# A cross-attention kernel whose statements are all put into another order

## The chip, the cores and the metric

The kernel runs on one NeuronCore of a Trainium2 chip. The metric is device time in microseconds of one launch that does the whole computation; the kernel before takes 1358.28 us (median of 3 runs, 1357.85 to 1358.52). The core's engines run at the same time, each its own instructions in order: TensorE (PE, with weight loads PEld), VectorE (DVE), ScalarE (ACT), GpSimd (POOL), and SyncE (SP), which only issues transfers here. They wait for one another through semaphores.

## What is computed

Cross-attention of 64 batches, in float32. x holds 256 rows of 512 for each batch, the context c 256 rows of 384.

```python
Q = layer_norm(x @ W_text + b_text, g1, beta1)        # 256 x 512
V = c @ W_audio + b_audio                             # 256 x 512
K = layer_norm(V, g2, beta2)
alpha = softmax(Q @ K.T / sqrt(512))                  # 256 x 256
H = (alpha @ V) @ W_out + b_out
out = layer_norm(H + x, g_out, beta_out)
```

The kernel folds W_audio @ W_out into one matrix (`wao`), so that the output is alpha @ c @ wao plus a bias row.

## The kernel before, in words

Batches are worked on one behind the other in a pipeline. A first part written out by hand takes batches up to 5 into the pipeline, then 58 steady rounds run (`for b in range(3, B - 3)`, line 1825), then an end written out by hand empties it. In round b five batches are in work: `q2` and `k2` project batch b+2; `at` is the attention of batch b up to the softmax; `last` (b-1) takes alpha @ c; `old` (b-2) multiplies with `wao` and adds x (`y` is its product); `settled` (b-3) does the last layer norm.

Nearly every matrix product is computed with fewer block products than the plain way, from sums and differences of blocks. The query projection is a `Fork` of 7 block products (`one` to `seven`, line 733); the key projection and the output product are `Thirds` of 15 products of 171 columns (`one` to `five`, line 557), whose blocks M, L, T, U, N lie in three PSUM banks, and between whose groups VectorE or ScalarE moves partial sums (`copy_n1`, `start_t`, `copy_t`, `start_l0`, `start_l1`, `take_m`, `start_u`). The scores are 7 parts (`score_part`, line 884), the context 7 parts and 2 plain products (`z_part`, line 1000, `context_two`, line 1062). The operands' sums are made mostly by GpSimd (`query_step`, `key_step`, `c_step`, `e_step`, `cs[..].add`, `x_new.add`, `z_step`).

The names that the prediction's steps touch:

- `at.add_p7(0)` and `(1)` (line 541): VectorE adds the kept seventh score part to scores in PSUM. `score_part(5)` waits for the first of them.
- `settled.shift(t)` (line 1261) and `settled.settle(t)` (line 1270): VectorE's two passes of the last layer norm over a row tile of 512; both read two tensors in SBUF: the row and a vector.
- `turn_c`, `turn_x`, `turn_e`, `k.turn`, `q.turn` (lines 76 and 520): VectorE turns 32x32 squares; the transfer that loaded them has put the squares in place.
- `y.one` needs all `z_step`s that make its operands; `y.three` needs `y.start_t`, and that `y.copy_n1` on ScalarE; `y.five` needs `y.take_m`.
- `store_e`, `fetch_e`: alpha goes to DRAM and comes back as squares (`ed`, `eq`); the same for keys (`kd`, `kq`) and queries (`qd`, `qq`).

The order is the order of the statements: the compiler's own scheduling is switched off (`tc.manual_schedule()`), every engine runs its instructions as the program issues them, and the first thing that waits holds up what stands behind it on its engine. All transfers in the rounds are issued on SP's queue, also in order. So a statement's place sets both where it stands on its own engine and what it stands behind.

Of the kernel before, what the change touches and what calls it, by code (L numbers as in the profile page):

```python
# [15 lines left out]
P = 128  # L16
# [6 lines left out]
def kernel(  # L23
# [1288 lines left out]

    keep_busy(6)
    c_turn = RowTurn(c_0, AC, 'cT')
    c_turn.tile(0)
    c_turn.tile(1)
    k[0] = Projection('k', 0, c_turn.T, wa_sb, ba_sb, AC, ST, bank[0:2])
    k[0].multiply(0, [0])
    k[0].multiply(1, [0])
    war = []  # L1320
    pool, tag = (once, 'e')
    war.append(pool.tile([P, HC, P], F32, tag=tag, name=f'war_{0}'))
    arrange(war[0], wa_sb[:, 0, :], HC, nc.gpsimd.tensor_copy)
    mean_wa = means(wa_sb, AC, 'mwa')
    k[0].multiply(0, [1])
    k[0].multiply(0, [2])
    k[0].multiply(1, [1])
    x_turn = RowTurn(x_0, DC, 'xT')
    x_turn.tile(0)
    k[0].multiply(1, [2])  # L1330
    pool, tag = (work, 'eT')
    war.append(pool.tile([P, HC, P], F32, tag=tag, name=f'war_{1}'))
    arrange(war[1], wa_sb[:, 1, :], HC, nc.gpsimd.tensor_copy)
    x_turn.tile(1)
    mean_wt = means(wt_sb, DC, 'mwt')
    pool, tag = (work, 'eT')
    war.append(pool.tile([P, HC, P], F32, tag=tag, name=f'war_{2}'))
    arrange(war[2], wa_sb[:, 2, :], HC, nc.gpsimd.tensor_copy)
    centre(wa_sb, mean_wa, AC)
    wa_t = const.tile([P, 11, WP], F32, tag='wa_thirds', name='wa_thirds')  # L1340
    third_weights(wa_sb, wa_t, [0])
    turn_weights(0, 1)
    k[0].evict(0)
    k[0].evict(1)
    q[0] = Projection('q', 0, x_turn.T, wt_sb, bt_sb, DC, LT, bank[2:4])
    q[0].multiply(0, [0])
    q[0].multiply(0, [1])
    cT[1] = turn_c(1)
    turn_weights(1, 1)
    bt_row = bt_sb.rearrange('p (o h) -> p o h', o=1)  # L1350
    mean_bt = means(bt_row, 1, 'mbt')
    q[0].multiply(1, [0])
    q[0].multiply(1, [1])
    k[0].scales()
    k[0].normalise([0])
    q[0].multiply(0, [2])
    q[0].multiply(0, [3])
    q[0].multiply(1, [2])
    q[0].multiply(1, [3])
    k[0].normalise([1])  # L1360
    k[0].store()
    turn_weights(2, 1)
    centre(wt_sb, mean_wt, DC)
    wt_blocks = weight_sums(wt_sb, DC // 2, 'wtsum')
    turn_weights(3, 1)
    centre(bt_row, mean_bt, 1)
    k[1] = Projection('k', 1, cT.pop(1), wa_sb, ba_sb, AC, ST, bank[4:6])
    k[1].multiply(0, [0])
    q[0].evict(0)
    q[0].evict(1)  # L1370
    k[1].multiply(0, [1])
    q[0].scales()
    xT[1] = turn_x(1)
    k[1].multiply(0, [2])
    k[1].multiply(1, [0])
    ba_row = ba_sb.rearrange('p (o h) -> p o h', o=1)
    mean_ba = means(ba_row, 1, 'mba')
    load_c(2)
    k[1].multiply(1, [1])
    fold_multiply(1, 0, 1)  # L1380
    fold_multiply(0, 0, 1)
    q[0].normalise([0])
    q[0].normalise([1])
    q[0].store()
    k[1].multiply(1, [2])
    bt_step = const.tile([P, H2], F32, tag='bt_step', name='bt_step')
    nc.vector.tensor_tensor(bt_step, bt_sb[:, :H2], bt_sb[:, H2:], ALU.subtract)
    g1_sb, be1_sb, g2_sb, be2_sb, bac_sb = take_columns()
    fold_multiply(1, 1, 2)
    fold_multiply(1, 2, 3)  # L1390
    load_x(2)
    centre(ba_row, mean_ba, 1)
    xs_1 = SumX(xT.pop(1), nc.vector)
    xs_1.add(1)
    fold_multiply(1, 3, 4)
    k[1].evict(0)
    Fork.seed()
    xs_1.add(1)
    k[1].evict(1)
    part = bias_parts()  # L1400
    xs[1] = xs_1
    q[1] = Fork(1, xs.pop(1).of, wt_blocks)
    q[1].one()
    q[1].seven()
    xs_1.add(1)
    k[1].square()
    wa_blocks = third_weights(wa_sb, wa_t, [3])
    q[1].after_one()
    fold_multiply(0, 1, 2)
    q[1].six()  # L1410
    ba_delta = third_bias(ba_sb, 'ba_delta')
    bias_rest(part, 1, 2)
    nc.vector.tensor_scalar(g2_sb, g2_sb, scale, None, ALU.mult)
    k[1].scales()
    k[1].normalise([0])
    cT[2] = turn_c(2)
    cs[2] = Sides(cT.pop(2), 'csum')
    cs[2].add(1)
    k[0].fetch()
    xs_1.add(1)  # L1420
    q[0].fetch()
    q[1].after_seven()
    q[1].start_q3()
    folds.append(p_at.tile([P, H], F32, tag='at', name='ps_fold'))
    fold_multiply(2, 0, 1)
    cs[2].add(1)
    cs[2].add(1)
    fold_multiply(0, 2, 3)
    cs[2].add(1)
    cs[2].add(1)  # L1430
    q[1].step_r()
    q[1].five()
    k[1].normalise([1])
    nc.vector.tensor_scalar(be2_sb, be2_sb, scale, None, ALU.mult)
    cs[2].add(1)
    q[1].after_five()
    xT[2] = turn_x(2)
    cs[2].add(1)
    fold_multiply(0, 3, 4)
    xs[2] = SumX(xT.pop(2))  # L1440
    xs[2].add(1)
    k2_0 = k[2] = Thirds('k', 2, cs.pop(2), wa_blocks, ba_sb, ba_delta)
    k2_0.one()
    q[1].three()
    fold_evict(1)
    k[1].store()
    fold_evict(0)
    q[1].two()
    k2_0.copy_n1()
    Thirds.seed_with(ba_sb)  # L1450
    q[1].four()
    at_0 = att[0] = Attention(0)
    at_0.k.turn()
    k2_0.start_t()
    fold_multiply(2, 1, 2)
    fold_multiply(2, 2, 3)
    q[1].square()
    q[1].scales()
    bias_rest(part, 2, 3)
    q[1].normalise([0])  # L1460
    Fork.seed()
    at_0.q.turn()
# [362 lines left out]
    for b in range(3, B - 3):  # L1825
# [95 lines left out]
        if b + 4 < B: load_c(b + 4)  # L1921
# [34 lines left out]
        if b + 4 < B: load_x(b + 4)  # L1956
# [394 lines left out]
```

## Time and profile before

| | |
|---|---|
| time of the runs shown | 1358.28 us, 1357.85 to 1358.52 |
| span of the profiled execution | 1355.6 us |
| TensorE busy in the span | 1343.8 us (99%), 8473 matmul records |
| VectorE, ScalarE, GpSimd busy | 1266.0, 1181.1, 1105.2 us |
| granted TensorE clock | 0.998 |
| DMA | 322.20 MB, 238 GB/s on average |

The profiled execution's own time is its span of 1355.6 us, first to last instruction, and what lies around it, which the profile does not show; the median of the runs is 2.7 us above the span. A float32 matmul leaves two records. A row of the list in order of time has the start, the time from the first start to the last end, engine, line, operation, tiles (buffer numbers left out), shapes and count; what stands in brackets is idle time before it and who ended it.

### The profile page before, as it was taken

The page shows a single profiled execution, that of the slowest core. Times are in us where ns is not written, and L with a number is a line of the kernel's source. Part 1 is how long each engine was busy: PE and PEld are TensorE (multiplying, and loading weights), DVE is VectorE, ACT ScalarE, POOL GpSimd, SP SyncE. Part 2 cuts the span into 40 slices and gives each one's busy share as a digit, 9 for nine tenths or more (in the row PEclk, how much of TensorE's full clock was granted, in tenths as well). Part 3 has the DMA queues.
Part 4 walks back from the last instruction along what each step waited for, and adds up shares of the span by engine and source line. Part 5 has one row for each costly group of instructions (what it writes and reads, how often), then busy time and mean ns, then how long its engine had stood idle before and what let it go on. Part 6 is the DMA issues. An engine that isn't in the chain of part 4 may idle for free.

```text
span 1355.6 us, 29587 instructions
## 1 busy us (share of the span) xinstructions
PE 1343.8 (99%) x8473; PEld 1240.2 (91%) x8473; DVE 1266.0 (93%) x3308; ACT 1181.1 (87%) x3304; POOL 1105.2 (82%) x1838
## 2 busy tenths in 40 slices
PE   9999999999999999999999999999999999999997
PEld 5889999999999999999999999999999999999996
DVE  6769999999999999999999999999999999999968
ACT  5788898898898988988988988989889888989885
POOL 5768888888888888888888888888888888888844
PEclk9999999999999999999999999999999999999999
DMA  9998889988888889888888888898888888888782
GB/s 219 235 252 227 242 236 250 245 238 241 250 240 248 238 244 250 236 241 248 238 244 245 238 242 246 237 255 241 242 247 233 248 242 241 246 247 242 213 252 87
DMA packets 449112, 322.20 MB, mean 238 GB/s; under 512 B 153781, under 2 KB 381621, under 8 KB 448950
## 3 DMA queue, kind: packets, MB, share of 16 engines
q1 hardware_dynamic: 448854, 320.20, 85.7%
q8 instruction: 67, 1.10, 0.4%
q14 instruction: 95, 0.78, 0.2%
q10 hardware_dynamic: 96, 0.13, 0.0%
HBM read 203.57 MB, written 116.65 MB: 236 GB/s over the span
## 4 chain that ended last, share of the span: by engine, by line
PE 97%; DVE 1%; DMA 1%; ACT 0%; issue 0%; SPq 0%; POOL 0%; DVEq 0%; POOLq 0%
PE ps_f L733 28%; PE ps_m L557 16%; PE ps_sc L884 14%; PE ps_n L557 11%; PE ps_u L557 8%; PE ps_z L1000 7%; PE ps_l L557 5%; PE ps_z L1062 5%; PE ps_sc L823 2%; DMA eq<-ed 0%; PE ps_f L440 0%; DVE yr L1261 0%; DMA c<-in_ctx_dram 0%; PE ps_l L244 0%; PE ps_u L440 0%
## 5 line engine op out<-in xcount | busy, mean ns | idle before, releaser
L733 PE MATMUL ps_f<-wtsum,xsum 128*128 128x256 f32 x756 | 194.0, 379 | 0.0
L352 POOL TENSOR_TENSOR csum<-csum,cT 128x256 f32<-128x256 f32 x310 | 173.3, 567 | 5.1
L733 PEld LDWEIGHTS ps_f<-wtsum,xsum 128*128 128x128 f32 x756 | 136.3, 190 | 14.5 <-issue 0.8
L527 ACT ACTIVATE qT<-qT,columns 128x256 f32<-128x256 f32 x256 | 147.6, 602 | 0.5 <-DVE qT L76 0.5
L527 ACT ACTIVATE kT<-kT,columns 128x256 f32<-128x256 f32 x256 | 147.4, 602 | 0.0
L884 PE MATMUL ps_sc<-kT,qT 128*128 128x128 f32 x928 | 133.1, 276 | 0.0
L1261 DVE SCALAR_TENSOR_TENSOR yr<-yr,nm,go 128x512 f32<-128x512 f32 x124 | 131.6, 1062 | 0.0
L733 PE MATMUL ps_f<-wt,xT 128*128 128x256 f32 x504 | 129.5, 379 | 0.0
L884 PEld LDWEIGHTS ps_sc<-kT,qT 128*128 128x128 f32 x928 | 119.3, 191 | 1.0
L869 POOL TENSOR_TENSOR qsum<-qT 128x256 f32<-128x256 f32 x116 | 84.6, 729 | 40.4 <-ACT qT L527 40.4
L866 POOL TENSOR_TENSOR ksum<-kT 128x512 f32<-128x512 f32 x58 | 74.0, 1276 | 52.1 <-ACT kT L527 52.1
L884 PE MATMUL ps_sc<-ksum,qsum 128*128 128x128 f32 x696 | 111.4, 283 | 0.1
L884 PEld LDWEIGHTS ps_sc<-ksum,qsum 128*128 128x128 f32 x696 | 93.6, 191 | 16.0 <-DVE ps_sc L541 15.7
L1270 DVE SCALAR_TENSOR_TENSOR yr<-yr,rstd,beo 128x512 f32<-128x512 f32 x120 | 103.9, 866 | 0.0
L541 DVE TENSOR_TENSOR ps_l<-ps_m,t 128x171 f32<-128x171 f32 x248 | 83.2, 336 | 20.0 <-ACT t L605 14.9
L990 POOL TENSOR_TENSOR esum<-eT 128x256 f32<-128x256 f32 x58 | 42.2, 728 | 72.1 <-DVE eT L76 69.8
L733 PEld LDWEIGHTS ps_f<-wt,xT 128*128 128x128 f32 x504 | 91.1, 190 | 10.2 <-issue 0.5
L488 ACT ACTIVATE kr<-kr,rstd 128x512 f32<-128x512 f32 x126 | 91.5, 727 | 0.1
L1125 ACT ACTIVATE junk<-yr,nm 128x512 f32<-128x512 f32 x124 | 89.1, 719 | 2.1 <-POOL nm L1107 2.0
L314 POOL TENSOR_TENSOR xsum<-xT 128x256 f32<-128x256 f32 x124 | 88.0, 731 | 2.2 <-DVE xT L76 2.2
L1062 PE MATMUL ps_z<-eT,c 128*128 128x256 f32 x304 | 86.7, 380 | 0.6 <-PE ps_u L557 0.6
L520 DVE STREAM_TRANSPOSE kT<-kq 128x512 f32<-128x512 f32 x122 | 84.0, 690 | 1.6 <-DMA kq<-kd 1.6
(284 smaller groups left out, 4648.7 us busy)
## 6 DMA issues: line engine op xcount, KB each, us to landing
kd<-kr SPq DMA_DIRECT2D x64, 512.0 KB, 3.2
qd<-qr SPq DMA_DIRECT2D x64, 512.0 KB, 2.9
kq<-kd SPq DMA_DIRECT2D x256, 128.0 KB, 3.0
qq<-qd SPq DMA_DIRECT2D x256, 128.0 KB, 3.2
xq<-in_x_dram SPq DMA_DIRECT2D x252, 128.0 KB, 4.6
x<-in_x_dram SPq DMA_DIRECT2D x63, 512.0 KB, 5.2
out_dram<-yr SPq DMA_DIRECT2D x62, 512.0 KB, 4.7
cq<-in_ctx_dram SPq DMA_DIRECT2D x252, 96.0 KB, 3.9
```

Of the source, the lines that this page charges most:

```text
L314: self.engine.tensor_tensor(*step)
L352: nc.gpsimd.tensor_tensor(*step)
L488: nc.scalar.mul(row, row, self.r[t])
L527: nc.scalar.activation(self.T[:, k, :], self.T[:, k, :], AF.Identity, bias=bet[:, k : k + 1], scale=gam[:, k : k + 1],)
L557: nc.tensor.matmul(place, lhsT=self.sides.of[n], rhs=self.weights[n], start=(n == 14), stop=True, skip_group_check=True,)
L733: nc.tensor.matmul(place, lhsT=side, rhs=w, start=(n == 7 and c == 0), stop=True, skip_group_check=True,)
L884: nc.tensor.matmul(self.place(t, m), lhsT=self.qsides[n][:, c], rhs=self.ksides[n][:, c], start=False, stop=True, skip_group_check=True,)
L1000: nc.tensor.matmul(self.zp[{1: 0, 2: 0, 4: 2}.get(n, 1)], lhsT=self.asides[n], rhs=self.bsides[n], start=(n == 7), stop=True, skip_group_c ...
L1062: nc.tensor.matmul(ps, lhsT=c_rows[self.b][:, s, bass.ts(j, P)], rhs=self.eT[:, s, :], start=start, stop=(s == ST - 1), skip_group_check=True,
L1125: nc.scalar.activation(junk, self.y[:, t, :], AF.Square, bias=self.nm[:, t : t + 1], accum_out=self.ssq[:, t : t + 1],)
L1261: nc.vector.scalar_tensor_tensor(row, row, self.nm[:, t : t + 1], go_sb, ALU.add, ALU.mult)
L1270: nc.vector.scalar_tensor_tensor(self.y[:, t, :], self.y[:, t, :], self.r[t], beo_sb, ALU.mult, ALU.add)
```

## The change

All statements of the first part, of the steady round and of the end stand in another order. Each engine has as many instructions of each kind and shape as before. One statement is written differently: the object of the next batch's attention, `Attention(b + 1)`, is made at the top of the round and called `nxt`; making it takes the batch's query and key objects out of two tables. The diff, cut to the parts that are spoken of below ("..." marks what is left out):

```diff
     keep_busy(6)
...
+    k[0] = Projection('k', 0, c_turn.T, wa_sb, ba_sb, AC, ST, bank[0:2])
...
     k[0].multiply(0, [0])
...
+    k[0].multiply(0, [1])
...
+    k[0].multiply(0, [2])
...
     k[0].multiply(1, [0])
...
-    k[0].multiply(0, [1])
-    k[0].multiply(0, [2])
...
+    fold_multiply(0, 0, 1)
...
-    fold_multiply(0, 0, 1)
...
     for b in range(3, B - 3):
         at = att[b]
         settled, old, last = att.pop(b - 3), att[b - 2], att[b - 1]
+        nxt = att[b + 1] = Attention(b + 1)
         k2 = k[b + 2] = Thirds("k", b + 2, cs.pop(b + 2), wa_blocks, ba_sb, ba_delta)
         q2 = q[b + 2]
         x_old = x_rows[b - 2]
...
+        k2.two()
+        k2.start_t()
+        at.open_scores()
+        q2.start_q3()
+        old.z_step(2)
+        k2.three()
+        settled.totals()
+        old.z_step(3)
+        last.fetch_e()
+        k2.copy_t()
+        q2.step_r()
+        at.affine_queries(2)
+        settled.deviation(0)
         last.context_sums()
         last.c_step(0)
...
-        old.z_step(4)
-        old.z_step(3)
+        at.query_step(1)
...
+        k2.start_u()
+        xT[b + 3] = turn_x(b + 3)
+        k2.five()
...
-        k2.start_u()
-        k2.five()
-        settled.shift(1)
-        k2.copy_n()
-        last.c_step(2)
-        k[b + 1].turn([0])
-        last.fetch_e()
+        cs[b + 3] = Sides(cT.pop(b + 3), "csum").add(1)
+        q2.four()
+        k2.leave_ends()
         k2.copy_u()
-        k2.leave_ends()
-        y.seed()
-        last.c_step(3)
-        q2.four()
-        old.z_step(5)
-        at.query_step(2)
-        q2.square(var[:, :2], [1])
         k2.middle_v()
         k2.leave_middle()
         k2.middle_less()
-        old.z_step(6)
-        settled.shift(0)
-        last.turn_e()
+        nxt.k.turn([0])
+        at.score_part(6)
+        old.z_step(5)
+        y.seed()
+        q2.square(var[:, :2], [1])
+        at.add_p7(0)
         k2.leave()
...
-        y.one()
-        at.score_part(6)
-        cs[b + 3].add(1)
         if done: done.store()
         done = settled
+        settled.shift(1)
+        cs[b + 3].add(1)
+        y.one()
+        q2.three()
+        settled.shift(0)
+        k2.square(var[:, 2:], [0])
+        k2.square(var[:, 2:], [1])
+        at.score_part(5)
+        last.turn_e()
+        at.query_step(3)
+        cs[b + 3].add(1)
         last.weight_sums()
         last.e_step(0)
-        at.add_p7(0)
         y.copy_n1()
+        q2.square(var[:, :2], [0])
+        y.two()
         y.start_t()
-        k2.square(var[:, 2:], [1])
-        q2.three()
-        at.score_part(5)
-        xT[b + 3] = turn_x(b + 3)
         at.add_p7(1)
-        if b + 4 < B: load_c(b + 4)
-        q2.square(var[:, :2], [0])
+        load_x_rows(b - 1)
         y.three()
+        at.score_part(2)
+        settled.settle(0)
...
-        y.start_l1()
-        y.start_l0()
-        settled.settle(1)
-        at.query_step(3)
-        at.score_part(4)
-        q[b + 1].turn()
...
+        y.take_m()
+        k2.normalise([1])
+        at.exponentials([0])
+        last.e_step(2)
+        y.start_u()
...
+        q2.fetch()
+        at.divide_e([0])
+        at.store_e()
+        last.z_part(2)
+        k2.seed()
+        k2.fetch()
...
         y.last_10()
+        y.last_00()
+        if b + 4 < B: nxt.key_step(1)
+        last.add_c21()
+        settled.settle(1)
+        if b + 4 < B: nxt.key_step(2)
         last.copy_top()
-        at.divide_e([1])
...
+    end.evict(0, stats=False)
+    end.evict_halves(1, [0])
+    end.evict_halves(1, [1])
+    end.statistics(0, 1)
...
+    end.shift(0)
...
-    end.evict_halves(1, [0])
-    end.shift(0)
-    end.evict_halves(1, [1])
```

The instructions of three places in a steady round, as each engine gets them. First VectorE, from the three sums that finish a key projection (`d`, `kr`) on; `yr` at L1261 is a `shift`, `eT`, `xT` and `kT` are transposes, `ps_sc` is `add_p7`, `ps_u<-ps_n` is `y.start_t`. Before:

```order
L541 TENSOR_TENSOR d<-ps_n,u 128x171
L541 TENSOR_TENSOR kr_3868<-ps_u,u 128x171
L541 TENSOR_TENSOR kr_3868<-d,ps_n 128x171
L1051 TENSOR_TENSOR zsum<-zsum,ps_z_3839 128x128
L1261 SCALAR_TENSOR_TENSOR yr_3600<-yr_3600,nm,go 128x512
L76 STREAM_TRANSPOSE eT_3980<-eq_3958 128x8x2x32
L541 TENSOR_TENSOR ps_sc<-ps_sc,sc_3925 128x128
L541 TENSOR_TENSOR ps_u<-ps_n,n_3997 128x171
L76 STREAM_TRANSPOSE xT_4006<-xq_3787 128x8x4x32
L541 TENSOR_TENSOR ps_sc<-ps_sc,sc_3925 128x128
```

and now:

```order
L541 TENSOR_TENSOR d<-ps_n,u 128x171
L541 TENSOR_TENSOR kr_3868<-ps_u,u 128x171
L541 TENSOR_TENSOR kr_3868<-d,ps_n 128x171
L520 STREAM_TRANSPOSE kT_3970<-kq_3846 128x4x4x32
L541 TENSOR_TENSOR ps_sc<-ps_sc,sc_3931 128x128
L1261 SCALAR_TENSOR_TENSOR yr_3595<-yr_3595,nm,go 128x512 x2
L76 STREAM_TRANSPOSE eT_3996<-eq_3904 128x8x2x32
L541 TENSOR_TENSOR ps_u<-ps_n,n_4002 128x171
L541 TENSOR_TENSOR ps_sc<-ps_sc,sc_3931 128x128
```

`add_p7(0)` has moved ahead of both shifts and of the transpose of e, the transpose of x has left the stretch (it stands earlier now), and `y.start_t` stands behind both shifts.

Second TensorE in the same stretch, from `q2.four` on; `ps_f` are query products, `ps_n<-wao` is `y.one`, `ps_u<-wao_thirds` is `y.three`, `ps_m<-wao` is `y.two`, `ps_sc` are score parts. Before:

```order
L733 MATMUL ps_f_91<-wtsum,xT_3727 128x256 x2
L733 MATMUL ps_f_90<-wt,xT_3727 128x256 x2
L557 MATMUL ps_n<-wao,zsum 128x171 x2
L884 MATMUL ps_sc<-ksum,qsum 128x128 x2
L733 MATMUL ps_f_90<-wt,xsum 128x256 x2
L884 MATMUL ps_sc<-ksum,qsum 128x128 x2
L557 MATMUL ps_u<-wao_thirds,zsum 128x171
L1000 MATMUL ps_z_4018<-esum,asum 128x128
L557 MATMUL ps_m<-wao,zsum 128x171 x2
L884 MATMUL ps_sc<-kT_3677,qT_3758 128x128 x4
```

and now:

```order
L733 MATMUL ps_f_91<-wtsum,xT_3666 128x256 x2
L884 MATMUL ps_sc<-ksum,qsum 128x128 x2
L733 MATMUL ps_f_90<-wt,xT_3666 128x256 x2
L557 MATMUL ps_n<-wao,zsum 128x171 x2
L733 MATMUL ps_f_90<-wt,xsum 128x256 x2
L884 MATMUL ps_sc<-ksum,qsum 128x128 x2
L557 MATMUL ps_m<-wao,zsum 128x171 x2
L557 MATMUL ps_u<-wao_thirds,zsum 128x171
L884 MATMUL ps_sc<-kT_3691,qT_3801 128x128 x6
L1000 MATMUL ps_z_4035<-esum,asum 128x128
```

Score part 6 comes ahead of a query product and of `y.one`; score part 5, the second `ps_sc` row, keeps its place behind the same amount of work; the context part (`ps_z`) has moved behind the scores.

Third GpSimd, from the query sum of `query_step(1)` to the first sum on alpha (`esum<-eT`), which waits for VectorE's transpose of e. Before:

```order
L869 TENSOR_TENSOR qsum<-qT_3758 128x256
L352 TENSOR_TENSOR csum<-cT_3921 128x256
L987 TENSOR_TENSOR asum<-asum,c_3773 128x128
L987 TENSOR_TENSOR c_3773<-c_3773,asum 128x128
L1051 TENSOR_TENSOR zsum<-zsum,zT 128x128
L869 TENSOR_TENSOR qsum<-qsum,qT_3758 128x256
L352 TENSOR_TENSOR csum<-csum,cT_3921 128x256 x2
L990 TENSOR_TENSOR esum<-eT_3980 128x256
```

and now:

```order
L869 TENSOR_TENSOR qsum<-qT_3801 128x256
L987 TENSOR_TENSOR asum<-c_3777 128x128
L869 TENSOR_TENSOR qsum<-qsum,qT_3801 128x256
L352 TENSOR_TENSOR csum<-cT_3926 128x256
L1051 TENSOR_TENSOR zsum<-zsum,zT 128x128
L352 TENSOR_TENSOR csum<-csum,cT_3926 128x256
L869 TENSOR_TENSOR qT_3801<-qT_3801,qsum 128x2x128
L352 TENSOR_TENSOR csum<-csum,cT_3926 128x256
L990 TENSOR_TENSOR esum<-eT_3996 128x256
```

Two context sums (`asum<-asum,c` and `c<-c`) have left the stretch ahead of the wait; the first context sum (`asum<-c`), which stood ahead of the query sum, and another query sum (`qT<-qT,qsum`) have come into it. The output product's sum (`zsum`, of `z_step(5)`) stands behind three sums of the stretch in both orders.

More of the change, by code (lines that the diff above doesn't have):

```diff
@@ L1443 @@
-    k2_0.one()
-    q[1].three()
-    fold_evict(1)
[L1446 to L1461, printed above, removed]
-    at_0.q.turn()
-    at_0.affine_queries(2)
-    fold_multiply(2, 3, 4)
-    xs[2].add(1)
```

1417 lines of the change are left out of this document (705 added, 712 removed).

## The prediction

> **What bounds the kernel now.** I read the page's busy times first, then the steady rounds as one window, then one round instruction by instruction on each engine.
>
> ```profile
> PE 1343.8 (99%) x8473; PEld 1240.2 (91%) x8473; DVE 1266.0 (93%) x3308; ACT 1181.1 (87%) x3304; POOL 1105.2 (82%) x1838
> 116.78:1250.64 1133.86, 1133.80 (x7372) 1063.33 (x7370) 1099.24 (x2916) 1012.95 (x2861) 962.35 (x1596) 1.00 0.88 243
> ```
>
> The second row (stretch, its length, then the busy time of TensorE, its weight loads, VectorE, ScalarE and POOL) covers 55 of the 58 steady rounds: 1133.86 / 55 = 20.62 us each. TensorE looks full, but a matmul's modelled end lies behind the next one's start, so short holes do not show as idle time; starts have to be read. VectorE is busy 1099.24 / 55 = 19.99 us of the 20.62, nearly as full. Here is one round of TensorE, from its first matmul at 611.97 to the next round's at 632.60 (start, duration):
>
> ```profile
> 611.97 1.03 PE L733 MATMUL ps_f<-wtsum,xsum 128*128 128x256 f32 x4
> 616.04 1.03 PE L733 MATMUL ps_f<-wtsum,xsum 128*128 128x256 f32 x4
> 616.90 0.45 PE L557 MATMUL ps_u<-wa_thirds,csum 128*128 128x171 f32 x2
> 617.19 0.74 PE L557 MATMUL ps_m<-wa_thirds,csum 128*128 128x171 f32 x4
> 621.53 0.81 PE L557 MATMUL ps_n<-wao,zsum 128*128 128x171 f32 x4
> 622.18 0.61 PE L884 MATMUL ps_sc<-ksum,qsum 128*128 128x128 f32 x4
> 622.62 1.03 PE L733 MATMUL ps_f<-wt,xsum 128*128 128x256 f32 x4
> 623.55 0.71 PE L884 MATMUL ps_sc<-ksum,qsum 128*128 128x128 f32 x4
> 624.10 0.46 PE L557 MATMUL ps_u<-wao_thirds,zsum 128*128 128x171 f32 x2
> 629.03 0.82 PE L557 MATMUL ps_m<-wao_thirds,zT 128*128 128x171 f32 x4
> 629.69 0.45 PE L557 MATMUL ps_u<-wao_thirds,zT 128*128 128x171 f32 x2
> 631.95 0.38 PE L1000 MATMUL ps_z<-esum,c 128*128 128x128 f32 x2
> 632.17 0.60 PE L1062 MATMUL ps_z<-eT,c 128*128 128x256 f32 x2
> 632.60 0.38 PE L733 MATMUL ps_f<-wtsum,xsum 128*128 128x256 f32 x1
> ```
>
> From start to start, undisturbed: a query product of two chunks (L733 x4, 616.04 to 616.90) takes 0.865 on average of its rows; one product of thirds (L557, two records) 0.29; a score part (L884 x4, 622.18 to 622.62) 0.44; a context part (L1000 x2) 0.22; a full context product (L1062 x2) 0.43. A round has 7, 30, 7, 7 and 2 of these: 6.06 + 8.70 + 3.08 + 1.54 + 0.86 = 20.24 us. So 20.62 contains 0.38 us of holes, and three are visible. `y.one` (621.53) takes 0.65 instead of 0.58. The score part at 623.55 starts 0.07 late (622.62 + 0.865 = 623.48) and takes 0.55 instead of 0.44. Half of `y.five` (629.03) takes 0.66 instead of 0.58. The waits of the weight loads name who is late at the largest hole, and the chain of waits holds a round without holes:
>
> ```profile
> PEld ps_sc L884 <- DVE ps_sc L541: 15.7, 53, 0.5
> 888.13 1.73 PE ps_f L733 x8
> 908.88 1.73 PE ps_f L733 x8
> 929.17 1.73 PE ps_f L733 x8
> ```
>
> The three starts are the same products one round apart: after a round of 20.75, in which something was late, the next takes 929.17 - 908.88 = 20.29. I take that as the price of a round whose waits all end early. What is late in the other rounds is `add_p7(0)`, the VectorE sum that score part 5 needs:
>
> ```profile
> 618.60 1.04 DVE L1261 SCALAR_TENSOR_TENSOR yr<-yr,nm,go 128x512 f32<-128x512 f32 x1
> 621.50 1.18 DVE L1261 SCALAR_TENSOR_TENSOR yr<-yr,nm,go 128x512 f32<-128x512 f32 x1
> 622.60 0.70 DVE L76 STREAM_TRANSPOSE eT<-eq 128x512 f32<-128x512 f32 x1
> 623.23 0.26 DVE L541 TENSOR_TENSOR ps_sc<-ps_sc,sc 128x128 f32<-128x128 f32 x1
> 623.65 1.22 DVE L76 STREAM_TRANSPOSE xT<-xq 128x1024 f32<-128x1024 f32 x1
> 626.18 1.02 DVE L1270 SCALAR_TENSOR_TENSOR yr<-yr,rstd,beo 128x512 f32<-128x512 f32 x1
> 630.61 0.74 DVE L1270 SCALAR_TENSOR_TENSOR yr<-yr,rstd,beo 128x512 f32<-128x512 f32 x1
> ```
>
> Its operand from score part 6 was issued by 622.62; the sum stands behind both `shift`s and the transpose of e and ends at 623.49, when TensorE has wanted it already. On VectorE the next instruction starts about 0.07 before the last one's end (622.60 + 0.70 against 623.23); I call duration less 0.07 an instruction's spacing.
>
> **The change, part by part.** No work is added or removed: only order moves, so every term is a hole closed or opened. Positions count from the round's first matmul (611.97 is 0). The reader of a matmul starts 0.2 after its issue has ended: the products of u end by the sum at 7.82, that is 619.79, and their copy starts at 620.00:
>
> ```profile
> 620.00 0.30 ACT L631 COPY u<-ps_u 128x171 f32<-128x171 f32 x1 [0.42 <-PE ps_u L557]
> 621.07 0.31 DVE L541 TENSOR_TENSOR kr<-d,ps_n 128x171 f32<-128x171 f32 x1
> 619.56 0.70 DVE L520 STREAM_TRANSPOSE kT<-kq 128x512 f32<-128x512 f32 x1
> ```
>
> *Score part 5.* Up to `start_u` VectorE's instructions stay nearly the same, so it is again free at 618.60, position 6.63. Then come the transpose of x (1.15), which ends before u arrives, `leave_ends`, three sums on u, half a transpose of the keys and `add_p7(0)`. u is there at 8.33; three sums at 0.24 end at 9.08, the half transpose (0.63) at 9.71, `add_p7(0)` at 9.97. Score part 5 stands at 11.44 on TensorE, as before, since what precedes it sums to the same. 1.4 us of room replace the hole: 0.07 + 0.11 = 0.18 a round.
>
> *y.one.* It writes into block N, which the last of the three sums on u (`kr<-d,ps_n`, 621.07 to 621.38) still reads; its weight load goes ahead of the matmul at 621.53. In the new order that sum ends at 9.15 and `y.one`, now behind score part 6, stands at 9.99: 0.07. *y.five.* Its M products overwrite what `start_u` reads:
>
> ```profile
> 628.61 0.34 DVE L541 TENSOR_TENSOR ps_u<-ps_m,m 128x171 f32<-128x171 f32 x1
> ```
>
> The sum ends at 628.95, the products start at 629.03. In the new order `y.four` stands at 14.29, VectorE takes M from 15.36 to 15.70, `start_u` ends near 16.05, and since z part 1 now lies between, the M products start at 16.54: 0.08. The three together: 0.33 a round, 20.62 to 20.29, the round of the chain above.
>
> *What is late next: y.three.* `y.start_t`, which it needs, now stands behind both shifts and the transpose of e. `y.three` is at 12.46. From 9.89 (the spacing of `add_p7(0)`) there follow two shifts, 0.63 of transpose, and `start_t`, 0.33 long. What the shifts cost decides:
>
> ```profile
> L1261 DVE SCALAR_TENSOR_TENSOR yr<-yr,nm,go x124: 711/1037/1756, 102.8 to 1344.3; 128x512 f32<-128x512 f32 x124
> 619.04 0.90 POOL L1051 TENSOR_TENSOR zsum<-zsum,zT 128x128 f32<-128x128 f32 x1
> 623.45 0.73 POOL L990 TENSOR_TENSOR esum<-eT 128x256 f32<-128x256 f32 x1 [1.31 <-DVE eT L76]
> ```
>
> The fastest of the 124 shifts took 0.71, the two of this round 1.04 and 1.18, both beside POOL work; the POOL sum under the first took 0.90, more than the 0.73 of one with twice its columns. So shift and POOL sum slow each other. In the old order POOL idles from 622.14 (10.17; 623.45 - 1.31) until e is turned. In the new one two asum steps come after that wait (about 0.4 each, an estimate from half of 0.73), a query step of about 0.7 comes before it, and the slowed sum meets no shift (about -0.45): 10.17 - 0.8 + 0.7 - 0.45 = 9.6. POOL then waits just while the shifts run, 9.89 to 11.2. e is turned by 11.84, `start_t` ends at 12.17, 0.29 before 12.46. I cost it at nothing, with that cover. Without it the shifts take 0.97 + 1.11, `start_t` ends at 12.93, and TensorE loses about 0.5. The Trainium skill, "SBUF — State Buffer", section "Who interferes with whom", says that a VectorE instruction with two SBUF inputs and a GpSimd instruction that reads SBUF exclude each other for the whole instruction. By that rule each shift could wait out a whole sum, 0.71 + 0.73, the loss would be 1.1 a round and the first rival below would end near 1403; the rows show 1.04 to 1.18, a shorter wait.
>
> *The round's seam.* `settle(1)` moves to the very end, ahead of the z sums and the `start_t` on which `k2.three` at 2.89 rests. z part 3, the last context part, is readable at 20.44, `add_c21` is done by 20.65, the settle takes 0.95 beside POOL's key sums (as at 626.18), to 1.36 in the next round. Then:
>
> ```profile
> 613.25 0.62 DVE L1051 TENSOR_TENSOR zsum<-ps_z,zT 128x256 f32<-128x256 f32 x2
> 614.12 0.34 DVE L541 TENSOR_TENSOR ps_u<-ps_n,n 128x171 f32<-128x171 f32 x1
> ```
>
> The three z sums take 614.12 - 613.25 = 0.87, to 2.23; `start_t` ends at 2.57: 0.32 of room. Nothing; with a settle as long as the longest shift, 1.76, it would be 0.5.
>
> *VectorE's load.* Shifts from 2.22 to 1.42, the second settle from 0.74 to 1.02: 19.99 - 0.52 = 19.5, so VectorE does not become the bound of a round of 20.3. *Transfers.* e is fetched a little earlier in the round, the x rows later, still a round ahead of their use. Nothing for both; a late e costs up to what it cost the round of 20.75, 0.1, where it occurs.
>
> *First rounds and end.*
>
> ```profile
> 0.00:50.00 50.00, 47.38 (x171) 29.26 (x172) 33.44 (x66) 29.34 (x69) 27.78 (x52) 1.00 0.94 224
> 7.53 1.17 POOL L179 COPY war<-wa 128x512 f32<-128x512 f32 x2 [1.16 <-DMA wa<-in_L_xattn_W_audio_dram]
> 25.22 1.10 PE L244 MATMUL ps_l<-wo,waT 128*128 128x512 f32 x2 [0.49 <-issue]
> 1348.32 0.75 DVE L1261 SCALAR_TENSOR_TENSOR y<-y,nm,go 128x512 f32<-128x512 f32 x1 [0.79 <-ACT junk L1142]
> ```
>
> In the first 50 us TensorE has 2.6 us of idle to win back. Key projection 0 now wants wa's second chunk one product earlier, about 0.6 before it lands at 7.5: +0.6; the first fold, which waited 0.49 at 25.22, comes one product later: -0.5. The rest of the start is dealt anew; bounds are -2 (that idle) and +6 (four shifts' worth of new waits at 1.5 each); I take +1, nearer the lower end because the products keep their rough sequence. At the end the last half row is evicted in the 0.79 that VectorE idled: -0.5 (bounds -0.8, and +2 should one wait on VectorE move onto the last store's chain).
>
> **Sum.** The execution spans 1355.6, the median is 1358.28; the 2.7 between stay. 58 rounds at 0.30 (of 0.33, the rest left for late transfers) give -17.4; with +1 and -0.5: 1358.3 - 16.9 = 1341.4. Forecast 1342 us.
>
> **The rivals.**
> 1. *y.three waits* (slower). If POOL is not idle at 9.9, or e lands late, a new 0.5 takes the place of the 0.33 won: 58 x 0.17 = +10, 1368 us. It decides for slower once `start_t` ends more than 0.33 after 12.46. For it: one chain on one engine with 0.29 to spare. Against it: the POOL count leaves 0.3, and one slow shift alone costs 0.1 or so.
> 2. *Half the gain.* One place (the seam, `y.three`, or the start with +6) eats 0.15 a round: 1342 + 8 = 1350. For it: rooms of 0.3 are small where a weight load goes ahead of its matmul.
> 3. *VectorE is the bound already*, and TensorE's holes only show it; new waits on VectorE keep the round: 1357. For it 19.99 of 20.62, against it the round of 20.29 and the cheaper shifts.
>
> That the attention object is made earlier does nothing by itself: it takes names out of tables, and no instruction comes of it.
>
> **How the numbers follow.** Forecast 0.60 (its own range 1337 to 1346), half the gain 0.18, no change 0.08, slower 0.14. 0.2% (2.7 us) is about what a measurement can tell from no change. Faster: 0.60 + 0.18 + 0.02 of the third; same 0.06; slower 0.14. The range takes the first two cases and reaches the third: 1336 to 1357.
>
> **What would show it.** Right: rounds of 20.3; no weight load of `ps_sc` waiting for VectorE's L541; L1261 with a median near 0.72; POOL's wait for eT longer than 1.31; both settles near 1.0. Wrong: weight loads of `ps_u<-wao_thirds` waiting for VectorE behind the transpose of e (first rival); rounds near 20.6 with VectorE at 97% (third); rounds of 20.3 but a loop that begins late would put the fault in the start.

## The result: 0.990 of the time before, and the profile after

The changed kernel takes 1345.47 us (median of 4 runs, 1344.81 to 1346.06) beside 1358.4 us (4 runs): a ratio of 0.9902, interval 0.9888 to 0.9916. The profiled execution spans 1343.5 us instead of 1355.6. The forecast was 1342 and a range of 1336 to 1357.

The busy times on the page of the changed kernel:

```profile
PE 1330.7 (99%) x8473; PEld 1249.0 (93%) x8473; DVE 1255.5 (93%) x3308; ACT 1184.9 (88%) x3304; POOL 1095.6 (82%) x1838
```

They say little by themselves. The span has to be cut at the starts of steady rounds (the first matmul of a round, as in the prediction): the first part, 56 rounds, one more round, the end. Three stretches of the kernel before, and then of the changed one (stretch, its length, then the busy time of TensorE, its weight loads, VectorE, ScalarE and GpSimd):

```profile
0.00:96.21 96.21, 93.01 (x413) 70.95 (x414) 62.27 (x128) 70.81 (x178) 64.77 (x117) 1.00 0.96 233
116.78:1271.27 1154.49, 1154.43 (x7505) 1082.65 (x7504) 1119.28 (x2969) 1031.37 (x2913) 979.80 (x1625) 1.00 0.88 243
1292.17:1355.60 63.43, 55.21 (x289) 47.90 (x287) 46.02 (x115) 42.54 (x112) 28.87 (x43) 0.95 0.50 164
```

```profile
0.00:96.67 96.67, 94.63 (x413) 71.29 (x414) 65.24 (x127) 69.72 (x177) 63.15 (x113) 1.00 0.90 227
116.97:1255.62 1138.65, 1138.65 (x7506) 1090.84 (x7505) 1106.06 (x2969) 1036.20 (x2914) 970.03 (x1625) 1.00 0.92 247
1276.33:1343.50 67.17, 56.47 (x290) 47.86 (x288) 45.72 (x111) 41.81 (x112) 28.64 (x43) 0.97 0.47 153
```

A round fell from 1154.49 / 56 = 20.62 to 1138.65 / 56 = 20.33. All 58 rounds, from 96.21 to 1292.17 and from 96.67 to 1276.33, took 1195.96 and take 1179.66: -16.3. The first part is 0.46 longer. The end is 3.74 longer: 67.17 instead of 63.43. The sum is -12.1, the difference of the spans. So the rounds did what was forecast, and a quarter of their gain is lost again at the end.

One round of TensorE in the changed kernel, from 604.92 to 625.25 (list in order of time: start, duration):

```profile
604.92 1.03 PE L733 MATMUL ps_f<-wtsum,xsum 128*128 128x256 f32 x4
608.10 0.64 PE L884 MATMUL ps_sc<-kT,qT 128*128 128x128 f32 x4
608.57 0.61 PE L884 MATMUL ps_sc<-ksum,qsum 128*128 128x128 f32 x4
614.96 0.74 PE L557 MATMUL ps_n<-wao,zsum 128*128 128x171 f32 x4
615.54 1.03 PE L733 MATMUL ps_f<-wt,xsum 128*128 128x256 f32 x4
616.40 0.61 PE L884 MATMUL ps_sc<-ksum,qsum 128*128 128x128 f32 x4
616.85 0.75 PE L557 MATMUL ps_m<-wao,zsum 128*128 128x171 f32 x4
617.43 0.45 PE L557 MATMUL ps_u<-wao_thirds,zsum 128*128 128x171 f32 x2
617.72 1.50 PE L884 MATMUL ps_sc<-kT,qT 128*128 128x128 f32 x12
619.06 0.39 PE L1000 MATMUL ps_z<-esum,asum 128*128 128x128 f32 x2
621.54 0.74 PE L557 MATMUL ps_m<-wao_thirds,zT 128*128 128x171 f32 x4
622.12 0.31 PE L557 MATMUL ps_u<-wao_thirds,zT 128*128 128x171 f32 x1
625.25 1.03 PE L733 MATMUL ps_f<-wtsum,xsum 128*128 128x256 f32 x4
```

The three holes are gone. `y.one` takes 615.54 - 614.96 = 0.58, score part 5 stands right behind its query product and takes 616.85 - 616.40 = 0.45, the M products of `y.five` take 0.58. `y.three` takes 617.72 - 617.43 = 0.29 and waits for nothing. One small hole is new: score part 1 (608.10) takes 0.47 instead of 0.44.

VectorE and GpSimd beside it. Their rows show the order that the prediction reckoned with: the sum, both shifts (one row, x2), the transpose of e, `start_t`; then, at the seam, the settle, ahead of the z sums and the next `start_t`:

```profile
614.68 0.27 DVE L541 TENSOR_TENSOR ps_sc<-ps_sc,sc 128x128 f32<-128x128 f32 x1
614.86 1.39 DVE L1261 SCALAR_TENSOR_TENSOR yr<-yr,nm,go 128x512 f32<-128x512 f32 x2
616.17 0.70 DVE L76 STREAM_TRANSPOSE eT<-eq 128x512 f32<-128x512 f32 x1
616.80 0.31 DVE L541 TENSOR_TENSOR ps_u<-ps_n,n 128x171 f32<-128x171 f32 x1
625.66 1.21 DVE L1270 SCALAR_TENSOR_TENSOR yr<-yr,rstd,beo 128x512 f32<-128x512 f32 x1
627.64 0.33 DVE L541 TENSOR_TENSOR ps_u<-ps_n,n 128x171 f32<-128x171 f32 x1
```

```profile
613.69 0.74 POOL L352 TENSOR_TENSOR csum<-csum,cT 128x256 f32<-128x256 f32 x1
616.95 0.73 POOL L990 TENSOR_TENSOR esum<-eT 128x256 f32<-128x256 f32 x1 [2.52 <-DVE eT L76]
```

GpSimd waits from 614.43 to 616.95, and the shifts run inside that wait. Over the whole run, in the view of the line's instructions (shortest, median, longest in ns):

```profile
L1261 DVE SCALAR_TENSOR_TENSOR yr<-yr,nm,go x124: 720/741/991, 106.6 to 1331.4; 128x512 f32<-128x512 f32 x124
L1270 DVE SCALAR_TENSOR_TENSOR yr<-yr,rstd,beo x120: 724/976/1447, 109.0 to 1316.9; 128x512 f32<-128x512 f32 x120
```

And the three largest holes of TensorE in the end, which the kernel before does not have:

```profile
1300.42 1.99 PE L1062 MATMUL ps_z<-eT,c 128*128 128x256 f32 x8 [0.68 <-ACT eT L951]
1304.84 0.53 PE L557 MATMUL ps_u<-wao_thirds,zsum 128*128 128x171 f32 x2 [0.98 <-POOL nm L1107]
1314.53 0.82 PE L557 MATMUL ps_n<-wao,csum 128*128 128x171 f32 x4 [1.50 <-DVE yr L707]
```

### The profile page after: what moved, and what is told of

Read it like the earlier page. It is cut to its first block, busy times and chain, and to the rows that moved or that the text cites. A ratio compares the mean times of both kernels' runs of the same rounds, so it can differ in the third digit from the quotient of the medians.

```text
span 1343.5 us, 29594 instructions
## 1 busy us (share of the span) xinstructions
PE 1330.7 (99%) x8473; PEld 1249.0 (93%) x8473; DVE 1255.5 (93%) x3308; ACT 1184.9 (88%) x3304; POOL 1095.6 (82%) x1838
## 4 chain that ended last, share of the span: by engine, by line
PE 97%; DMA 1%; DVE 1%; issue 0%; ACT 0%; SPq 0%; POOL 0%; DVEq 0%; ACTq 0%; POOLq 0%
PE ps_f L733 28%; PE ps_m L557 16%; PE ps_sc L884 13%; PE ps_n L557 10%; PE ps_u L557 8%; PE ps_z L1000 7%; PE ps_l L557 5%; PE ps_z L1062 5%; PE ps_sc L823 1%; PE ps_f L440 0%; DMA qd<-qr 0%; DMA qq<-qd 0%; PE ps_m L440 0%; SPq L73 0%; PE ps_m L244 0%
## 5 line engine op out<-in xcount | busy, mean ns | idle before, releaser
L527 ACT ACTIVATE qT<-qT,columns 128x256 f32<-128x256 f32 x256 | 154.2, 605 | 2.4 <-DVE qT L76 2.4
L527 ACT ACTIVATE kT<-kT,columns 128x256 f32<-128x256 f32 x256 | 134.8, 613 | 0.5 <-DVE rden L923 0.5
L1270 DVE SCALAR_TENSOR_TENSOR yr<-yr,rstd,beo 128x512 f32<-128x512 f32 x120 | 128.4, 1070 | 0.0
L884 PE MATMUL ps_sc<-kT,qT 128*128 128x128 f32 x928 | 124.3, 277 | 0.0
L884 PEld LDWEIGHTS ps_sc<-kT,qT 128*128 128x128 f32 x928 | 114.6, 191 | 1.5
L884 PEld LDWEIGHTS ps_sc<-ksum,qsum 128*128 128x128 f32 x696 | 100.6, 191 | 6.0
L884 PE MATMUL ps_sc<-ksum,qsum 128*128 128x128 f32 x696 | 105.9, 275 | 0.0
L869 POOL TENSOR_TENSOR qsum<-qT 128x256 f32<-128x256 f32 x116 | 85.0, 732 | 18.1 <-DVE zsum L1051 17.3
L1261 DVE SCALAR_TENSOR_TENSOR yr<-yr,nm,go 128x512 f32<-128x512 f32 x124 | 86.9, 739 | 1.0 <-ACT junk L1125 1.0
L794 ACT ACTIVATE junk<-ps_f 128x512 f32<-128x512 f32 x126 | 75.4, 598 | 13.6 <-PE ps_f L733 2.4
L460 ACT ACTIVATE junk<-kr 128x512 f32<-128x512 f32 x126 | 79.4, 630 | 3.9
```

The lines of the kernel that those rows point to most:

```text
L527: nc.scalar.activation(self.T[:, k, :], self.T[:, k, :], AF.Identity, bias=bet[:, k : k + 1], scale=gam[:, k : k + 1],)
L884: nc.tensor.matmul(self.place(t, m), lhsT=self.qsides[n][:, c], rhs=self.ksides[n][:, c], start=False, stop=True, skip_group_check=True,)
L1261: nc.vector.scalar_tensor_tensor(row, row, self.nm[:, t : t + 1], go_sb, ALU.add, ALU.mult)
L1270: nc.vector.scalar_tensor_tensor(self.y[:, t, :], self.y[:, t, :], self.r[t], beo_sb, ALU.mult, ALU.add)
```

## The experiments

**Which part of the program gives and which takes.** First part, rounds and end can be exchanged, since each has the same statements in both kernels. Two kernels exchange the end, the first with the changed rounds:

```diff
-    k2_m3 = k[B - 1] = Thirds('k', B - 1, cs.pop(B - 1), wa_blocks, ba_sb, ba_delta)
-    settled, old, last = (att[B - 5], att[B - 4], att[B - 3])
...
+    settled_m3 = att.pop(B - 6)
+    settled_m3.totals()
...
```

> The changed kernel, but with the end of the kernel before (first part and steady rounds as changed). The trace of the changed kernel has its last round's start at 1276.33 and 67.17 us behind it; in the kernel before 63.43 lie behind the same place. Theory (the end's own order costs it): the part behind the last round's start is 63.4 again, the span falls by 3.7 to 1339.8, the time from 1345.5 to about 1341.7. Rival (the new rounds hand the end later operands, and the order of the end has nothing to do with it): the end stays at 67 and the time at 1345.5.

The other has the opposite exchange, in the kernel before:

> The kernel before, but with the end of the changed one. Theory (the end's own order costs it): 63.43 becomes about 67.2 and the time 1358.4 + 3.7 = 1362.1. Rival (it is the new rounds that spoil the end): 63.4 stays, less 0.7 for the earlier last evictions, and the time is 1357.7.

1342.46 us (1341.7 to 1343.0) and 1362.14 (1360.67 to 1364.52), beside 1359.8 for the kernel before on that chip: ratios 0.9878 (0.9863 to 0.9893) and 1.002 (1.0011 to 1.0029). So the second kernel lost 2.3 us where 3.7 were expected; that its time came out as written is chance, since the kernel before took 1.4 more on that chip. The stretch of the end, old end behind new rounds, then new end behind old rounds (the texts call its start, where all 58 rounds are done, the last round's start):

```profile
1276.59:1340.10 63.51, 55.21 (x290) 47.91 (x288) 45.95 (x111) 42.21 (x112) 29.47 (x43) 0.95 0.50 162
```

```profile
1293.84:1360.00 66.16, 56.20 (x289) 47.93 (x287) 45.29 (x115) 41.91 (x112) 29.16 (x43) 0.98 0.50 157
```

The end's own order costs time, whatever runs ahead of it: 3.7 behind the new rounds, 2.7 behind the old ones. About 1.0 of the 3.7 hangs on the rounds ahead, so the rival has a share: read from start to start, the largest hole is 1.1 behind the old rounds and 1.7 behind the new ones.

The third kernel takes first part and end from the kernel before, the rounds from the changed one, and only the place of the two last evictions from the new end:

```diff
     end.evict(0, stats=False)
     last.lift_rows(0, 1)
     last.lift_rows(1, 1)
+    end.evict_halves(1, [0])
+    end.evict_halves(1, [1])
     end.statistics(0, 1)
     last.store()
-    end.evict_halves(1, [0])
     end.shift(0)
-    end.evict_halves(1, [1])
```

> The new steady rounds between the first part and the end of the kernel before, with the two last evictions placed as in the changed kernel. Theory (the three parts add): first part to 96.2, 58 rounds at 20.33, 63.4 - 0.7 behind: span 96.2 + 1179.7 + 62.7 = 1338.6, time about 1341.0. Rival (parts fitted to one another, a seam costs): 1343 or more.

1341.83 us (1339.77 to 1343.48), ratio 0.9873 (0.9858 to 0.9888), with an end of 62.61:

```profile
1278.89:1341.50 62.61, 55.22 (x290) 47.91 (x288) 45.83 (x111) 42.21 (x112) 29.04 (x43) 0.96 0.50 164
```

In the median the parts add to within 1 us of the theory's 1341.0. The profiled execution took 1343.45: its end is as short as expected, but its rounds took 1278.89 - 95.95 = 1182.94, which is 3.3 longer than in the changed kernel, and the loss stands in a few rounds in which `y.three` waits. In three of them VectorE's first half transpose of the keys, which the new order puts right ahead of `add_p7(0)`, waits for its transfer. The longest case:

```profile
777.74 0.71 DVE L520 STREAM_TRANSPOSE kT<-kq 128x512 f32<-128x512 f32 x1 [1.20 <-DMA kq<-kd]
780.86 0.56 PE L557 MATMUL ps_u<-wao_thirds,zsum 128*128 128x171 f32 x2 [0.86 <-DVE ps_u L541]
```

So the chain that ends in `start_t` also hangs on that transfer; why it was late there is not shown. In this kernel and in the one with the old end alone every run lies below every run of the changed kernel (1344.81 at the least), and the medians 3 to 4 us below its; between the two the runs don't decide. The evictions' place is worth 63.51 - 62.61 = 0.9 of the end.

**What makes the end's largest hole.** GpSimd's bias additions stood in front of the late product:

```diff
-    add_bias(B - 1, [1])
...
-    add_bias(B - 2, [1])
...
     last.o.one()
+    add_bias(B - 1, [1])
+    add_bias(B - 2, [1])
```

> The changed kernel with two statements of the end moved: both bias additions that stand on GpSimd between the sums for the last-but-one output product (1.27 us each at 1310.47 and 1312.12) go behind that product's first group. The largest hole of the end, 1.67 us before the matmul at 1314.53, stands behind them. Theory (they hold it up): the hole goes, the time falls by 1.5 or so, to 1344.0. Rival (the product waits for something else as well, VectorE's or the eviction's): within 0.5 of 1345.5.

1345.69 us (1345.32 to 1346.72): nothing gained. The edit moves the additions at 1312.12 and 1313.76; the one at 1310.47 stays. Even so the last of the sums is done at 1312.73 now. The product still starts as late, and its row names VectorE:

```profile
1314.49 0.82 PE L557 MATMUL ps_n<-wao,csum 128*128 128x171 f32 x4 [1.31 <-DVE yr L707]
```

It overwrites blocks that VectorE still evicts for the batch before, and VectorE stood in front of a transfer, as two rows of the changed kernel show (the wait, and the last reading of block N):

```profile
1310.76 1.25 DVE L76 STREAM_TRANSPOSE qT<-qq 128x1024 f32<-128x1024 f32 x1 [2.04 <-DMA qq<-qd]
1314.06 0.32 DVE L707 SCALAR_TENSOR_TENSOR yr<-d,ps_n 128x170 f32<-128x170 f32 x1
```

So that transpose was moved behind the evictions, with the affine steps that read it:

```diff
-    q[B - 1].turn()
...
-    q[B - 1].affine(g1_sb, be1_sb, [1])
...
     old.o.last_00()
+    end.q.turn()
+    end.q.affine(g1_sb, be1_sb, [1])
+    end.q.affine(g1_sb, be1_sb, [0])
...
```

> The changed kernel with the last batch's query transpose and its four affine steps moved in the end, from ahead of the evictions of the last-but-two batch's output to behind them. In the changed kernel VectorE idles 1.85 us at 1310.7 for the transfer qq<-qd and then transposes for 1.25, while the blocks that the last-but-one product wants to overwrite wait to be read; that product starts 1.5 late at 1314.5. Theory (the transpose ahead of the evictions makes this hole): the evictions run about 1.25 earlier, the hole falls from 1.67 to 0.4, the part behind the last round's start from 67.2 to 65.9, the time to 1344.2. Rival (another operand of that product is late too, or the moved work opens as large a hole at the last scores): 1345.5 or more.

1346.51 us (1346.12 to 1347.29). The hole went, and the rival came: four affine steps now stand on ScalarE ahead of a copy of zT, and the next product waits for that.

```profile
1313.51 0.77 PE L557 MATMUL ps_n<-wao,csum 128*128 128x171 f32 x4
1317.15 1.13 PE L1159 MATMUL ps_f<-wao,zT 128*128 128x512 f32 x2 [1.16 <-ACT zT L1081]
```

The cause of that hole is settled, and moving these statements does not shorten the time. The causes of the other two holes are read from the trace only: the copy of the transposed e right ahead of its product, and `start_t` behind the maxima on VectorE, which ends at 1304.69 (the row names GpSimd, whose `nm` that product does not read).

**Is it the place of the sum, or VectorE's load?** The sum goes back behind the shifts and the transpose of e, in the changed kernel:

```diff
-        at.add_p7(0)
         k2.leave()
...
-        at.score_part(5)
         last.turn_e()
+        at.add_p7(0)
+        at.score_part(5)
```

> The changed kernel with add_p7(0) behind both shifts and the transpose of e, still ahead of score part 5. It would start near 11.7 and end near 11.95 in the round, where score part 5 stands at 11.44. Theory: TensorE waits about 0.6 there, and what follows (y.two, y.three) comes that much later and waits no more: rounds of 20.9, the time 1345.5 + 35 = 1380. Rival (the shorter shifts give the gain, whatever the place of the sum): 1345.5.

1382.26 us (1380.57 to 1384.4), as the theory had it, 36.8 / 58 = 0.63 a round more than the changed kernel, although the shifts stayed as short: their median is 742 ns in the view of the line. The waits of the weight loads (44.7 in 58 times) show the place:

```profile
PEld ps_sc L884 <- DVE ps_sc L541: 44.7, 58, 1.3
```

```profile
L1261 DVE SCALAR_TENSOR_TENSOR yr<-yr,nm,go x124: 706/742/999, 106.5 to 1368.0; 128x512 f32<-128x512 f32 x124
```

**Is the sum's place enough?** The sum alone was moved ahead of the transpose of e in the kernel before:

```diff
-        last.turn_e()
...
         at.score_part(6)
+        at.add_p7(0)
+        last.turn_e()
...
-        at.add_p7(0)
```

> The kernel before with two statements of the round moved: add_p7(0) goes directly behind score part 6, and the transpose of e behind it, so that on VectorE shift(0) is followed by the sum, then the transpose of e, then start_t. Score part 6 is readable at 622.82 in the round shown, the sum ends near 623.08, and score part 5 can start at 623.48; start_t ends as before near 623.75 or 0.2 later. Theory (the late sum makes the hole of score part 5): its 0.153 a round goes, rounds of 20.47, the time 1358.3 - 8.9 = 1349.4; if the transpose of e is late by the 0.2 that VectorE waits for score part 6, y.three takes back up to 0.1: 1355. Rival (VectorE's load of 19.99 bounds the round and is unchanged): 1358.3.

And with score part 6 earlier as well:

```diff
-        last.turn_e()
...
+        at.score_part(6)
+        at.add_p7(0)
+        last.turn_e()
         y.one()
-        at.score_part(6)
...
-        at.add_p7(0)
```

> The same with score part 6 ahead of y.one on TensorE, as in the changed kernel: y.one stands 0.44 later, and VectorE need not wait for the score part. Theory: the hole of y.one (0.064 a round) goes too, rounds of 20.41, the time 1358.3 - 12.6 = 1345.7; only y.five's 0.07 and the 0.02 of a score part are left of what the whole change closed. Rival (VectorE's load): 1358.3.

1384.47 us (1383.82 to 1387.15) and 1368.61 (1367.91 to 1370.26), beside 1359.05 for the kernel before on that chip: both slower, which neither the theory nor the rival had. The wait of score part 5 is gone, but others stand in its place. Waits of the weight loads with the sum moved alone and `y.three` in one of its rounds, then a round of the second kernel:

```profile
PEld ps_z L1000 <- POOL esum L990: 19.9, 58, 0.6
PEld ps_m L557 <- DVE ps_u L541: 6.8, 44, 0.2
529.88 0.56 PE L557 MATMUL ps_u<-wao_thirds,zsum 128*128 128x171 f32 x2
```

```profile
524.64 0.74 POOL L990 TENSOR_TENSOR esum<-eT 128x256 f32<-128x256 f32 x1 [1.51 <-PE ps_f L733]
524.87 0.47 PE L557 MATMUL ps_u<-wao_thirds,zsum 128*128 128x171 f32 x2
525.43 0.49 PE L1000 MATMUL ps_z<-esum,asum 128*128 128x128 f32 x2
```

With the sum moved alone VectorE waits 0.15 for score part 6, as the expectation allowed, and `start_t` comes later: `y.three` starts at 529.88 instead of 529.34 + 0.44 = 529.78 and its pair takes 0.56 instead of 0.45, a loss of 0.2 where 0.1 had been allowed. With score part 6 ahead of `y.one`, the second kernel, this loss is all but gone.

In both, the context part that reads `esum` waits. In the old order it stands right behind `y.three`, and whichever of the two goes first on VectorE, the sum or the transpose of e, the other is late. In the kernel before, the sum on e ends at 623.45 + 0.73 = 624.18, in time for its reader at 624.39. Here the transpose of e ends at 524.49 (the row of `esum` names TensorE, but transposed e is what it reads), the sum on e at 525.38, and its reader starts at 525.43 instead of 524.87 + 0.29 = 525.16.

In the changed kernel the same sum ends at 616.95 + 0.73 = 617.68, and TensorE comes to both readers later: `y.two` (0.58) has moved ahead of `y.three`, and three score parts (1.34) now stand ahead of the context part, which comes at 619.06. By these rows the move of `y.two` alone would nearly do for the context part, since right behind `y.three` it would stand at 617.72. No run makes either move alone; that TensorE's moves are what lets the sum go first is read from the rows, not shown.

**What the shifts' cover is worth.** Two of GpSimd's sums on x are put into its wait, beside the shifts:

```diff
+        x_new = SumX(xT.pop(b + 3))
+        x_new.add(1)
+        x_new.add(1)
         last.weight_sums()
...
-        x_new = SumX(xT.pop(b + 3))
-        x_new.add(1)
...
-        x_new.add(1)
```

> The changed kernel with GpSimd work put beside the shifts: the first two sums on x, 0.73 each, go ahead of the sums on e, into the 2.52 us in which GpSimd waits. Theory (the shifts are short because GpSimd does nothing beside them): both shifts take 1.0 or more, as in the kernel before, start_t ends near 12.9 instead of 12.20 and y.three, at 12.46, waits 0.3 to 0.5: rounds of 20.6 to 20.8, 1363 to 1374. Rival (the price of a shift does not hang on GpSimd): shifts at 0.73, time within 1 of 1345.5.

1380.5 us (1378.46 to 1382.01), ratio 1.0159 (1.0138 to 1.0181). VectorE, GpSimd and TensorE in a round that starts at 598.89, and the waits of the weight loads:

```profile
608.83 2.16 DVE L1261 SCALAR_TENSOR_TENSOR yr<-yr,nm,go 128x512 f32<-128x512 f32 x2
611.55 0.30 DVE L541 TENSOR_TENSOR ps_u<-ps_n,n 128x171 f32<-128x171 f32 x1
```

```profile
608.36 1.43 POOL L314 TENSOR_TENSOR xsum<-xT 128x256 f32<-128x256 f32 x2
```

```profile
611.91 0.56 PE L557 MATMUL ps_u<-wao_thirds,zsum 128*128 128x171 f32 x2 [0.34 <-DVE ps_u L541]
```

```profile
PEld ps_u L557 <- DVE ps_u L541: 34.2, 58, 0.6
```

The time lies above the range of the theory, whose mechanism the rows show. The shifts take 2.16 instead of 1.39, GpSimd's sums 1.43 as ever. `start_t` ends at 611.85, position 12.96, and TensorE loses 34.2 / 58 = 0.59 a round. In the changed kernel it ends at 616.80 + 0.31 - 604.92 = 12.19. The delay of 0.77 puts `y.three` at 611.91 - 598.89 = 13.02 instead of 617.43 - 604.92 = 12.51, about 0.5 later, so the room was about 0.27. The rest of the loss, 0.1, is in the product itself: its pair takes 0.56 instead of 0.45.

**Three that tested something else.** In these the sum crosses the score part itself in the program: ahead of part 6 in the first two, behind part 5 in the third. They compute other scores, and the waits turn round too, since the part named second now waits for the one named first.

```diff
+        at.add_p7(0)
         last.turn_e()
...
         at.score_part(6)
...
-        at.add_p7(0)
```

> The kernel before with one statement of the round moved: VectorE's add_p7(0) goes ahead of the transpose of e, behind shift(0). It would then start at 622.8 instead of 623.23 in the round shown, and end 0.4 before score part 5 can start at 623.48. Theory (the late sum makes the hole of score part 5): that hole, 0.055 + 0.098 a round, goes, rounds fall from 20.62 to 20.47, the time by 58 x 0.153 = 8.9 to 1349.5. Rival (VectorE's load bounds the round, 19.99 of 20.62, and it is unchanged here): 1358.4.

> The same, and score part 6 ahead of y.one on TensorE, so that y.one stands 0.44 later. Theory: the hole of y.one (0.064 a round) goes as well, rounds of 20.41, the time 1358.4 - 12.6 = 1345.8; y.five's 0.07 is left. Rival (VectorE's load): 1358.4; or y.copy_n1 and what hangs on it come 0.44 later and y.three waits: 1349 or more.

```diff
-        at.add_p7(0)
...
         at.score_part(5)
         last.turn_e()
+        at.add_p7(0)
```

> The changed kernel with add_p7(0) put back behind both shifts and the transpose of e. In the changed round it starts at 9.77 and ends at 10.04; behind them it starts near 11.7 and ends near 11.98, where score part 5 stands at 11.44. Theory: score part 5 waits about 0.6 and the y.three behind it finds its own operand in time, rounds near 20.9, the time 1345.5 + 58 x 0.6 = 1380. Rival (the gain is VectorE's cheaper shifts, and the place of the sum is nothing): the shifts stay at 0.73 and the time at 1345.5.

1397.73, 1431.0 and 1363.36 us. The first two (the second has score part 6 ahead of `y.one` too) make score part 6 wait for shift(0) and the sum, and say nothing on the theory. The third is of use: the sum waits for score part 5, `start_t` comes later behind it, and `y.three` waits 18.1 / 58 = 0.31 a round, a second look at the first rival's place:

```profile
PEld ps_u L557 <- DVE ps_u L541: 18.1, 58, 0.4
```

## Why the prediction was right, and where not

**The bound** was read rightly: holes on TensorE, not VectorE's load. VectorE's share of a round rose, from 1119.28 / 1154.49 = 96.9% to 1106.06 / 1138.65 = 97.1%, and the round still became shorter. The third rival falls with that, and with the sum put back: same work on VectorE, 37 us more.

**Score part 5, `y.one`, `y.five`.** All three closed, at the places forecast (the sum at 614.68 is position 9.76; 9.71 was worked out). They were put at 0.33 a round, from one round, and 0.30 of it went into the sum. Read from start to start over all 58 rounds they come to 0.15, 0.07 and 0.07 on average, 0.29, and 0.28 was won (16.3 / 58). For score part 5 the place of the sum is shown by the run that puts it back. The hole of `y.one` is gone too where score part 6 goes earlier in the old order (522.98 to 523.56, 0.58); for `y.five` the cause is read from the rows alone.

**`y.three`.** `start_t` was to end at 12.17 and ends at 12.19; nothing is lost. The room was to be 0.29, and 0.27 was measured. The price without the cover was to be 0.5 and measured 0.59: the product comes 0.5 later, and the 0.1 that a waiting pair takes longer was not reckoned with. One step was right by chance: the two shifts were to take 0.97 + 1.11 = 2.08 beside GpSimd, and took 2.16 - 0.07 = 2.09, but the first had the whole delay and the second none. The prediction reckoned with a late e, but not with the keys' transpose ahead of the sum waiting for its transfer, as it did in the kernel with the old first part and end.

**The seam.** The settle took 1.21 where 1.02 was expected, `start_t` ends at 627.97 instead of the equivalent of 627.82, and `k2.three` lost nothing. **VectorE's load** came to 19.75 a round (1106.06 / 56), not 19.5: both settles now run beside GpSimd, and the median of L1270 is 976.

**The first part** was to cost 1 and cost 0.46; behind the old first part the rounds began between 95.6 and 96.9 in these runs, so that term is within what one execution can tell.

**The end** is the step that failed. It was written as -0.5, with bounds of -0.8 and +2. The earlier place of the last evictions gave 0.9 where it was tried alone, but the stretch became 3.74 longer. The prediction priced the one place of the end where VectorE visibly idled and did not follow TensorE through the new order there. Read from start to start, the products of the old end follow one another with 0.1 us of holes in 55, so up to the last product another order could only lose; the new one has 4.6.

**What the prediction left out.** It treated the sum's move as a gain by itself. The two kernels that move the sum in the old order of TensorE lose 10 to 25 us. The change also moves `y.two` ahead of `y.three` and the context part behind the scores. The first stands in the prediction, as the place 12.46 of `y.three`, though not as a condition; of the context part, which needs the sum on e, it says nothing. That this reader was in time was luck as far as the prediction goes.

## What to carry to other kernels

Where an engine that works in order feeds the bounding one at several places, moving one item early makes another late: list what each reader then waits for, and look whether the reader can be moved too. Price every stretch of a reordered program on the bounding engine, the short end included: where that engine has no holes, another order can only lose. And keep the stretches apart that can be exchanged, so that the good ones can be put together.

## What the runs showed of the hardware

A shift and a sum of GpSimd's wait for each other whole; they do not share. Where GpSimd had nothing to do, a shift took 0.74. Beside two sums that follow on each other (608.36 to 609.79) the first of the two shifts had the whole delay:

```profile
L1261 DVE SCALAR_TENSOR_TENSOR yr<-yr,nm,go x124: 720/744/1531, 106.6 to 1365.1; 128x512 f32<-128x512 f32 x124
```

It took 2.16 - 0.65 = 1.5 (0.65 is the spacing of a free shift, 1.39 - 0.74), twice a free one, and both sums kept their 0.73. The rows of the kernel before say the same, although the prediction read them as two instructions that slow each other. The shifts at 618.60 and 621.50 lie beside these sums, neither of them longer than when alone:

```profile
618.63 0.45 POOL L987 TENSOR_TENSOR c<-c,asum 128x128 f32<-128x128 f32 x1
621.40 0.73 POOL L352 TENSOR_TENSOR csum<-csum,cT 128x256 f32<-128x256 f32 x1
```

Each shift ends 0.55 or 0.56 after the sum beside it (619.64 against 619.08, 622.68 against 622.13), as in the run with the two sums (610.34 against 609.79). The sum at 619.04, which took 0.90, came behind the shift and waited for it in its turn. These two shifts (1.04 and 1.18) waited only 0.3 and 0.5, because the first of the two sums is short and the second had begun before the shift.

The Trainium skill, "SBUF — State Buffer", section "Who interferes with whom", says that such a pair excludes each other for the whole instruction; the trace of this run agrees, and so do these rows of the kernel before, which the prediction had held against it. The section also says that the order of issue decides who waits; here the shift (608.83) waited for a sum that began after it, near 609.05, and the shift at 618.60 for the one at 618.63. The rows have starts and no issues, so they don't test this.

A product that waits for its operand pays a little more than the wait: in three of the runs above, the pairs at 611.91, 529.88 and 780.86 start late, and each takes 0.56 instead of 0.45.
